# Transposing one operand of a two-layer graph network on VectorE and the DMA engines instead of TensorE

## The chip, the cores and the metric

The kernel runs on one core of one Trainium2 chip. The metric is the device time of one execution in microseconds (us). Each figure below is the median of a kernel's timed executions.

## The reference, cut to what matters

```python
# x, adj: (32, 512, 512) fp32; 32 independent batches; nodemask: (32, 512)
# layer 0
h   = relu(layernorm(x))
agg = (adj @ h) / max(rowsum(adj), 1e-6)
x   = x + relu(concat([h, agg]) @ W0.T)          # W0: (512, 1024)
# layer 1
h   = relu(layernorm(x))
q, k = split(h @ Wqk);  v = h @ Wv
agg = adj @ (k * mask)
w   = mask * rowdot(q, agg) / sqrt(512)
x   = x + softmax(w over the 512 rows)[:, None] * v
```

## The kernel before

Each batch has six 512 x 512 x 512 products, under names that every profile line uses. Layer 0: **y** = h0 W2, and **o** = h0 W1 + A y, which is two products summed in one accumulation. Layer 1: **z** = A (h1 mask), **q** = h1 (Wq Wk^T), whose row-dot with z gives the attention weight, and **v** = h1 Wv. A is the adjacency with its rows divided by their sums.

A product is not done plainly. It is one step of the Strassen-Winograd scheme: 7 parts on 256-wide blocks instead of 8, at the price of sums of blocks. Four sums on VectorE prepare the left operand (their results are called `hT_s`, `aT_s`, `h1T_s`), and four prepare the right one (`h1m_t`, `y_t`):

```python
class Left:                         # tt = one VectorE tensor_tensor, 128x512
    ...
    tt(s1, a21, a22, ALU.add)       # first sum
    tt(a21, a11, a21, ALU.subtract) # second, in place
    tt(s2, s1, a11, ALU.subtract)   # third
    tt(s4, a12, s2, ALU.subtract)   # fourth
    self.p = {1: a11, 2: a12, 3: s4, 4: a22, 5: s1, 6: s2, 7: a21}
```

The parts run in the order 1, 6, 7, 5, 2, 4, 3. **Part 1 needs no sum; part 6, the second, needs the third sum.** After parts 6 and 7 VectorE makes u2 and u3 out of PSUM, and the later parts wait for those.

The kernel gives TensorE its left operands transposed. All three (h0 as `hT`, A as `aT`, h1 as `h1T`) are transposed on TensorE in 128 x 128 tiles, sixteen an operand (1.83 us of TensorE for h1's sixteen; `pth`, `pta`, `pt` are their PSUM tiles), and ScalarE copies them out (four copies of 128 x 512 an operand, 595 ns each):

```python
def transpose_block(dst, src, c, func, name):
    p = ps_t.tile([P, 4, P], F32, tag="t", name=name)
    for d in range(4):
        nc.tensor.transpose(p[:, d, :], src[:, ts(d, P)], ident)
    nc.scalar.activation(dst[:, :, ts(c, P)], p, func)
```

The loop is software-pipelined over the batches:

```python
for i in range(B + 1):
    layer0_y(i)
    transpose_h1(i - 1); mask_h1(i - 1)
    layer1_z(i - 1)
    transpose_adj(i)
    load_a(i + 1)                         # DMA of the next adj
    XN[0, i + 1] = layer_norm(i + 1)      # statistics on VectorE, power on GpSimd
    between = layer1_q(i - 1)
    layer0_out(i, between)
    transpose_h(i + 1); normalize_adj(i + 1)
    layer1_v(i - 1)
    load_x(i + 2)
    # (conditions for the first and last batches cut)
```

The source order is not the order in which an engine runs its instructions. A scheduler orders each engine's queue when the kernel is compiled, and what stands in front in a queue can hold up what stands behind: below, VectorE stays idle for 2.66 us before a sum whose operand is late, while sums whose operands have landed stand behind it.

Of the kernel before, what the change touches and what calls it, by code (L numbers as in the profile page):

```python
# [10 lines left out]
F32 = mybir.dt.float32  # L11
# [4 lines left out]
P = 128  # L16
# [6 lines left out]
def kernel(  # L23
# [42 lines left out]
    class Left:  # L66


        def __init__(self, t, name, tag):
            s = big.tile([P, 3, 2, H], F32, tag=tag, bufs=1, name=f"{name}_s")  # L70
            a11, a12, a21, a22 = block(t, 0, 0), block(t, 1, 0), block(t, 0, 1), block(t, 1, 1)
            s1, s2, s4 = s[:, 0], s[:, 1], s[:, 2]
            tt(s1, a21, a22, ALU.add)
            tt(a21, a11, a21, ALU.subtract)
            tt(s2, s1, a11, ALU.subtract)
            tt(s4, a12, s2, ALU.subtract)
            self.p = {1: a11, 2: a12, 3: s4, 4: a22, 5: s1, 6: s2, 7: a21}
# [15 lines left out]
    def product(name, pairs, sink, between=()):  # L93


        between = list(between)

        def part(k, bank, first):
            n = 0
            for rc in range(2):  # L100
                for left, right in pairs:
                    for dc in range(2):
                        nc.tensor.matmul(  # L103
                            bank[:, rc, :], left.p[k][:, dc, ts(rc, P)], right.p[k][:, dc, :],
                            start=(first and n == 0), stop=(n == 4 * len(pairs) - 1),
                            skip_group_check=True,
                        )
                        n += 1
            if between:
                between.pop(0)()  # L110

        def bank(k):
            return ps_m.tile([P, 2, H], F32, tag="m", name=f"p{name}_{k}")

        def temp(tag, bufs):
            return big.tile([P, 2, H], F32, tag=tag, bufs=bufs, name=f"{tag}{name}")

        p1 = bank(1)
        part(1, p1, True)
        s1 = temp("s1", 1)  # L120
        nc.scalar.activation(s1, p1, AF.Copy)  # L121
        p6 = bank(6)
        part(6, p6, True)
        u2 = temp("u2", 2)
        tt(u2, p6, s1, ALU.add)
        p7 = bank(7)
        part(7, p7, True)
        u3 = temp("u3", 2)
        tt(u3, p7, u2, ALU.add)
        p5 = bank(5)  # L130
        part(5, p5, True)
        sink(1, 1, p5, u3)
        part(2, p1, False)
        sink(0, 0, p1, None)
        part(4, p7, False)
        sink(1, 0, p7, u2)
        part(3, p5, False)
        sink(0, 1, p5, u2)
        for f in between:
            f()  # L140
# [6 lines left out]
                tt(block(dst, r, c), p, u, ALU.add)  # L147
        return sink

    def transpose_block(dst, src, c, func, name):  # L150

        p = ps_t.tile([P, 4, P], F32, tag="t", name=name)
        for d in range(4):
            nc.tensor.transpose(p[:, d, :], src[:, ts(d, P)], ident)  # L154
        nc.scalar.activation(dst[:, :, ts(c, P)], p, func)  # L155

    X, A, XN, HT, AT, Y, H1T, H1M, Z, DEGM, SM = ({} for _ in range(11))

    def load_x(b):
        X[b] = tile4("x", 3, f"x_{b}")  # L160
# [14 lines left out]
    load_x(0)  # L175
    w_in = []
    for half, tag, bufs in (
        (w0[:, 0:F], "x", 3), (w0[:, F:2 * F], "x", 3), (wqk[:, 0:F], "c", 3), (wqk[:, F:2 * F], "c", 3),
    ):
        t = tile4(tag, bufs, f"w_in{len(w_in)}")  # L180
        nc.sync.dma_start(out=t, in_=half.rearrange("(c p) f -> p c f", p=P))  # L181
        w_in.append(t)
# [13 lines left out]
    def layer_norm(b, name):  # L196

        mv = small.tile([P, C, 2], F32, tag="mv", name=f"mv{name}")
        rstd = small.tile([P, C], F32, tag="rstd", name=f"rstd{name}")
        for c in range(C):  # L200
            st = small.tile([P, 6], F32, tag="st", bufs=4, name=f"st{name}_{c}")
            nc.vector.bn_stats(st, X[b][:, c, :])  # L202
            nc.vector.bn_aggr(mv[:, c, :], st)
        nc.vector.tensor_scalar(rstd, mv[:, :, 1], LN_EPS, None, op0=ALU.add)  # L204
        nc.gpsimd.tensor_tensor(rstd, rstd, mhalf, op=ALU.pow)  # L205
        xn = tile4("xn", 2, f"xn{name}")
        for c in range(C):
            nc.vector.tensor_scalar(  # L208
                xn[:, c, :], X[b][:, c, :], mv[:, c, 0:1], rstd[:, c:c + 1],
                op0=ALU.subtract, op1=ALU.mult,  # L210
            )
        return xn

    def normalize_adj(b):
        deg = small.tile([P, C], F32, tag="deg", name=f"deg_{b}")
# [7 lines left out]
            nc.scalar.activation(A[b][:, c, :], A[b][:, c, :], AF.Copy, scale=rdeg[:, c:c + 1])  # L223

    def transpose_h(b):
        t = tile4("hT", 1, f"hT_{b}")
        xn = XN.pop((0, b))
        for c in range(C):
            transpose_block(t, xn[:, c, :], c, AF.Relu, f"pth_{b}_{c}")
        HT[b] = Left(t, f"hT_{b}", "hTs")  # L230

    def transpose_adj(b):
        t = tile4("aT", 1, f"aT_{b}")
        an = A.pop(b)
        for c in range(C):
            transpose_block(t, an[:, c, :], c, AF.Copy, f"pta_{b}_{c}")
        AT[b] = Left(t, f"aT_{b}", "aTs")

    def transpose_h1(b):
        t = tile4("h1T", 1, f"h1T_{b}")  # L240
        xn = XN[1, b]
        for c in range(C):
            transpose_block(t, xn[:, c, :], c, AF.Relu, f"pt1_{b}_{c}")
        H1T[b] = Left(t, f"h1T_{b}", "h1Ts")

    def mask_h1(b):
        t = tile4("h1m", 1, f"h1m_{b}")
        xn = XN[1, b]
        for c in range(C):
            nc.vector.tensor_scalar(t[:, c, :], xn[:, c, :], 0.0, mcol[:, c, b:b + 1], op0=ALU.max, op1=ALU.mult)  # L250
        H1M[b] = Right(t, f"h1m_{b}", big, "h1mt")

    def layer0_y(b):
        y = tile4("c", 3, f"y_{b}")
        product(f"y_{b}", [(HT[b], w2)], store_in(y))
        Y[b] = Right(y, f"y_{b}", big, "yt")

    def layer0_out(b, between):
        def sink(r, c, p, u):
            xb = block(X[b], r, c)  # L260
            if u is not None:
                t = big.tile([P, 2, H], F32, tag="pre", bufs=2, name=f"pre_{b}_{r}{c}")
                tt(t, p, u, ALU.add)
                p = t
            nc.vector.scalar_tensor_tensor(xb, p, 0.0, xb, op0=ALU.max, op1=ALU.add)

        product(f"o_{b}", [(HT.pop(b), w1), (AT[b], Y.pop(b))], sink, between)
        XN[1, b] = layer_norm(b, f"1_{b}")

    def layer1_z(b):  # L270
        Z[b] = tile4("c", 3, f"z_{b}")
        product(f"z_{b}", [(AT.pop(b), H1M.pop(b))], store_in(Z[b]))

    def layer1_q(b):

        q = tile4("c", 3, f"q_{b}")
        product(f"q_{b}", [(H1T[b], m)], store_in(q))
        z = Z.pop(b)
        w = small.tile([P, C], F32, tag="w", name=f"w_{b}")
        for c in range(C):  # L280
            nc.vector.scalar_tensor_tensor(
                q[:, c, :], q[:, c, :], 1.0, z[:, c, :], op0=ALU.mult, op1=ALU.mult, accum_out=w[:, c:c + 1],
            )
        nc.vector.tensor_tensor(w, w, DEGM.pop(b), op=ALU.mult)
        top = small.tile([P, 1], F32, tag="top", name=f"top_{b}")
        nc.vector.tensor_reduce(top, w, AX.X, ALU.max)
# [26 lines left out]
        return [lambda: None, lambda: None, maximum, spread, total]  # L313

    def layer1_v(b):
        v = tile4("c", 3, f"v_{b}")
        product(f"v_{b}", [(H1T.pop(b), w3)], store_in(v))
        xo, sm = X.pop(b), SM.pop(b)
        for c in range(C):
            nc.vector.scalar_tensor_tensor(  # L320
                xo[:, c, :], v[:, c, :], sm[:, c:c + 1], xo[:, c, :], op0=ALU.mult, op1=ALU.add
            )
        nc.sync.dma_start(out=out[b].rearrange("(c p) f -> p c f", p=P), in_=xo)


    XN[0, 0] = layer_norm(0, "0_0")
    mcol = const.tile([P, C, B], F32, name="mcol")
    pmk = ps_t.tile([P, C, B], F32, tag="t", name="pmk")
    for c in range(C):
# [2 lines left out]
    transpose_h(0)  # L332
    for t, dst in zip(w_in, (w1T, w2T, wqT, wkT)):
        for c in range(4):
            transpose_block(dst, t[:, c, :], c, AF.Copy, f"ptw_{dst.name}_{c}")
    for d in range(D):
        p = ps_m.tile([P, 512], F32, tag="m", name=f"pm_{d}")
        for a in range(D):
# [10 lines left out]
    for i in range(B + 1):  # L349
        between = []  # L350
        if i < B:
            layer0_y(i)
        if i > 0:
            transpose_h1(i - 1)
            mask_h1(i - 1)
            XN.pop((1, i - 1))
            layer1_z(i - 1)
        if i < B:
            transpose_adj(i)
        if i + 1 < B:  # L360
            load_a(i + 1)
            XN[0, i + 1] = layer_norm(i + 1, f"0_{i + 1}")
        if i > 0:
            between = layer1_q(i - 1)
        if i < B:
            layer0_out(i, between)
        else:
            for f in between:
                f()
        if i + 1 < B:  # L370
            transpose_h(i + 1)
            normalize_adj(i + 1)
        if i > 0:
            layer1_v(i - 1)
        if i + 2 < B:
            load_x(i + 2)
# [28 lines left out]
```

## Time and profile before

| kernel before | value | how to read it |
|---|---|---|
| time | 2618.59 us | median of 4 |
| TensorE busy | 98% of the span | it sets the end |
| VectorE, ScalarE busy | 63%, 18% | room on average, which says nothing about the moment |
| granted TensorE clock | 0.999 | no throttle in the loop |
| one batch | 79.89 us | from one `pta` to the next |

The prediction shows the page, the chain and the timeline. From the view of waits it used one more line (columns: who waits for whom, us in total, times, longest):

```profile
PE pv L103 <- DVE u3v L64: 22.5, 31, 0.8
```

Within the loop this is the only wait of TensorE that recurs: 0.73 us a batch, once in v. The last adjacency transposes and q's parts follow one another with no gap.

### The profile page before, as it was taken

The page shows a single profiled execution, that of the slowest core. Times are in us where ns is not written, and L with a number is a line of the kernel's source. Part 1 is how long each engine was busy: PE and PEld are TensorE (multiplying, and loading weights), DVE is VectorE, ACT ScalarE, POOL GpSimd, SP SyncE. Part 2 cuts the span into 40 slices and gives each one's busy share as a digit, 9 for nine tenths or more (in the row PEclk, how much of TensorE's full clock was granted, in tenths as well). Part 3 has the DMA queues.
Part 4 walks back from the last instruction along what each step waited for, and adds up shares of the span by engine and source line. Part 5 has one row for each costly group of instructions (what it writes and reads, how often), then busy time and mean ns, then how long its engine had stood idle before and what let it go on. Part 6 is the DMA issues. An engine that isn't in the chain of part 4 may idle for free.

```text
span 2616.5 us, 30420 instructions
## 1 busy us (share of the span) xinstructions
PE 2559.3 (98%) x12548; PEld 2218.6 (85%) x12548; DVE 1647.6 (63%) x3282; ACT 481.6 (18%) x854; POOL 74.3 (3%) x70
## 2 busy tenths in 40 slices
PE   6999999999999999999999999999999999999998
PEld 4888888888888888888888888888888888888887
DVE  4766567666576665676665766656766657666555
ACT  2211212111121112121111211121211112111211
POOL 0000000000000000000000000000000000000000
PEclk9999999999999999999999999999999999999999
DMA  4100111010111000110101110011101011100000
GB/s 146 33 33 30 35 49 49 33 49 17 49 49 49 33 33 33 49 49 33 49 17 49 49 49 33 33 33 49 49 33 49 17 49 49 49 33 33 33 17 33
DMA packets 53514, 107.91 MB, mean 41 GB/s; under 512 B 1632, under 2 KB 1632, under 8 KB 53376
## 3 DMA queue, kind: packets, MB, share of 16 engines
q1 hardware_dynamic: 53376, 105.98, 11.7%
q8 instruction: 98, 1.61, 0.3%
q14 instruction: 40, 0.33, 0.0%
HBM read 72.42 MB, written 33.55 MB: 41 GB/s over the span
## 4 chain that ended last, share of the span: by engine, by line
PE 97%; DVE 1%; DMA 0%; SPq 0%; ACT 0%; issue 0%; POOL 0%; POOLq 0%; DVEq 0%
PE po L103 30%; PE pz L103 15%; PE pq L103 15%; PE pv L103 15%; PE py L103 15%; PE pth L154 2%; PE pta L154 2%; PE pt L154 2%; DVE u3v L64 1%; PE pm L339 1%; DMA mask_sb<-in_nodemask_dram 0%; PE pbc L297 0%; DVE st L202 0%; SPq L181 0%; PE psum L307 0%
## 5 line engine op out<-in xcount | busy, mean ns | idle before, releaser
L103 PE MATMUL po<-w1T,hT 128*128 128x256 f32 x768 | 200.5, 383 | 0.0
L103 PE MATMUL po<-y,aT 128*128 128x256 f32 x768 | 197.1, 379 | 0.0
L103 PE MATMUL pv<-wv_sb,h1T 128*128 128x256 f32 x768 | 186.7, 379 | 0.0
L103 PE MATMUL pq<-m_sb,h1T 128*128 128x256 f32 x768 | 186.6, 379 | 0.0
L103 PE MATMUL pz<-h1m,aT 128*128 128x256 f32 x768 | 186.6, 379 | 0.0
L103 PE MATMUL py<-w2T,hT 128*128 128x256 f32 x768 | 181.7, 379 | 0.7 <-ACT s1y L121 0.7
L202 DVE BATCH_NORM_STATS2 st<-x 128x6 f32<-128x512 f32 x256 | 166.8, 674 | 9.6 <-DMA x<-in_x_dram 8.1
L208 DVE TENSOR_SCALAR xn<-x,mv,rstd 128x512 f32<-128x512 f32 x256 | 122.6, 543 | 66.3 <-POOL rstd L205 66.3
L103 PEld LDWEIGHTS py<-w2T,hT 128*128 128x128 f32 x768 | 145.7, 190 | 21.3 <-ACT s1y L121 1.1
L103 PEld LDWEIGHTS po<-y,aT 128*128 128x128 f32 x768 | 145.9, 190 | 19.8
L103 PEld LDWEIGHTS po<-w1T,hT 128*128 128x128 f32 x768 | 143.2, 190 | 18.6
L103 PEld LDWEIGHTS pv<-wv_sb,h1T 128*128 128x128 f32 x768 | 141.2, 190 | 16.7
L103 PEld LDWEIGHTS pq<-m_sb,h1T 128*128 128x128 f32 x768 | 141.1, 190 | 16.6
L103 PEld LDWEIGHTS pz<-h1m,aT 128*128 128x128 f32 x768 | 141.0, 190 | 16.6
L205 POOL TENSOR_TENSOR rstd<-rstd,mhalf 128x4 f32<-128x4 f32 x64 | 73.6, 1151 | 2488.5 <-DVE rstd L204 2488.5
L64 DVE TENSOR_TENSOR pre<-po,u2o 128x512 f32<-128x512 f32 x64 | 44.3, 692 | 149.9 <-PE po L103 149.9
L103 PE MATMUL po<-w_t,hT_s 128*128 128x256 f32 x512 | 131.5, 379 | 0.0
L103 PE MATMUL po<-y_t,aT_s 128*128 128x256 f32 x512 | 131.4, 379 | 0.0
L155 ACT ACTIVATE hT<-pth 128x512 f32<-128x512 f32 x128 | 69.8, 595 | 334.5 <-PE pth L154 334.4
L103 PE MATMUL pv<-wv_t,h1T_s 128*128 128x256 f32 x512 | 121.1, 379 | 0.0
L103 PE MATMUL pz<-h1m_t,aT_s 128*128 128x256 f32 x512 | 121.0, 379 | 0.0
L103 PE MATMUL pq<-m_t,h1T_s 128*128 128x256 f32 x512 | 121.0, 379 | 0.0
(151 smaller groups left out, 4389.3 us busy)
## 6 DMA issues: line engine op xcount, KB each, us to landing
x<-in_x_dram SPq DMA_DIRECT2D x32, 1024.0 KB, 5.3
adj<-in_adj_dram SPq DMA_DIRECT2D x32, 1024.0 KB, 5.2
out_dram<-x SPq DMA_DIRECT2D x32, 1024.0 KB, 4.3
w_in<-in_L_gnn_W_dram SPq DMA_DIRECT2D x2, 1024.0 KB, 9.0
w_in<-in_L_gnn_Wqk_dram SPq DMA_DIRECT2D x2, 1024.0 KB, 13.1
wv_sb<-in_L_gnn_Wv_dram SPq DMA_DIRECT2D x1, 1024.0 KB, 14.4
mask_sb<-in_nodemask_dram SPq DMA_DIRECT2D x1, 64.0 KB, 12.0
```

Of the source, the lines that this page charges most:

```text
L64: nc.vector.tensor_tensor(o, a, b, op=op)
L103: nc.tensor.matmul(bank[:, rc, :], left.p[k][:, dc, ts(rc, P)], right.p[k][:, dc, :], start=(first and n == 0), stop=(n == 4 * len(pairs) ...
L154: nc.tensor.transpose(p[:, d, :], src[:, ts(d, P)], ident)
L155: nc.scalar.activation(dst[:, :, ts(c, P)], p, func)
L202: nc.vector.bn_stats(st, X[b][:, c, :])
L205: nc.gpsimd.tensor_tensor(rstd, rstd, mhalf, op=ALU.pow)
L208: nc.vector.tensor_scalar(xn[:, c, :], X[b][:, c, :], mv[:, c, 0:1], rstd[:, c:c + 1], op0=ALU.subtract, op1=ALU.mult,)
L339: nc.tensor.matmul(p, wqT[:, a, ts(d, P)], wkT[:, a, :], start=(a == 0), stop=(a == D - 1))
```

## The change

Its intent is to take h1's sixteen transposes off TensorE, the bound. VectorE transposes h1 within 32 x 32 blocks, in place, in four instructions of 128 x 512. Then sixteen DMAs of 64 KB move the blocks between the four groups of 32 partitions. To pay for the new work on VectorE, ScalarE takes over the normalization (one activation with scale, bias and relu). q and v are no longer stored; they are consumed block by block out of PSUM. The first two edits of the diff only address the transposed operands in a new layout, in which the first index is the block of rows; it holds for all three.

```diff
-            a11, a12, a21, a22 = block(t, 0, 0), block(t, 1, 0), block(t, 0, 1), block(t, 1, 1)
+            a11, a12, a21, a22 = block(t, 0, 0), block(t, 0, 1), block(t, 1, 0), block(t, 1, 1)
...
-                            bank[:, rc, :], left.p[k][:, dc, ts(rc, P)], right.p[k][:, dc, :],
+                            bank[:, rc, :], left.p[k][:, rc, ts(dc, P)], right.p[k][:, dc, :],
...
+    def turn(t, src, name, how):
+        if how == "pe":
+            for c in range(C):
+                transpose_block(t[:, c, :].rearrange("p (d n) -> p d n", d=4), src[:, c, :], f"{name}_{c}")
+            return
+        for c in range(C):
+            nc.vector.transpose(src[:, c, :], src[:, c, :])
+        s16, t16 = (u.rearrange("p c (d n) -> p (c d) n", n=P) for u in (src, t))
+        for q in range(4):
+            for r in range(4):
+                nc.sync.dma_start(out=t16[ts(q, 32), :, ts(r, 32)], in_=s16[ts(r, 32), :, ts(q, 32)])
...  # layer_norm
-            nc.vector.tensor_scalar(
-                xn[:, c, :], X[b][:, c, :], mv[:, c, 0:1], rstd[:, c:c + 1],
-                op0=ALU.subtract, op1=ALU.mult,
-            )
+            nc.scalar.activation(h[:, c, :], X[b][:, c, :], AF.Relu, bias=nb[:, c:c + 1], scale=rstd[:, c:c + 1])
...  # transpose_h and transpose_adj: turn(..., "pe"); transpose_h1:
+            nc.vector.tensor_scalar(hm[:, c, :], h[:, c, :], mcol[:, c, b:b + 1], None, op0=ALU.mult)
         t = tile4("h1T", 1, f"h1T_{b}")
-        for c in range(C):
-            transpose_block(t, xn[:, c, :], c, AF.Relu, f"pt1_{b}_{c}")
+        turn(t, h, f"pt1_{b}", "dma")
+        H1M[b] = Right(hm, f"h1m_{b}", big, "h1mt")
         H1T[b] = Left(t, f"h1T_{b}", "h1Ts")
...  # q and v: the sink multiplies each block with z, or adds it to x, in 256-wide pieces
```

(The changes in the numbers of buffers are cut.)

More of the change, by code (lines that the diff above doesn't have):

```diff
@@ L66, with __init__ @@
     class Left:
-        def __init__(self, t, name, tag):
-            s = big.tile([P, 3, 2, H], F32, tag=tag, bufs=1, name=f"{name}_s")
-            a11, a12, a21, a22 = block(t, 0, 0), block(t, 1, 0), block(t, 0, 1), block(t, 1, 1)
+        def __init__(self, t, name, tag, bufs=1):
+            s = big.tile([P, 3, 2, H], F32, tag=tag, bufs=bufs, name=f"{name}_s")
+            a11, a12, a21, a22 = block(t, 0, 0), block(t, 0, 1), block(t, 1, 0), block(t, 1, 1)
             s1, s2, s4 = s[:, 0], s[:, 1], s[:, 2]
@@ L123, in product @@
         part(6, p6, True)
-        u2 = temp("u2", 2)
+        u2 = temp("u2", 1)
         tt(u2, p6, s1, ALU.add)
@@ L127, in product @@
         part(7, p7, True)
-        u3 = temp("u3", 2)
+        u3 = temp("u3", 1)
         tt(u3, p7, u2, ALU.add)
@@ L148, in store_in, with transpose_block @@
         return sink
-    def transpose_block(dst, src, c, func, name):
+    def transpose_block(dst, src, name):
         p = ps_t.tile([P, 4, P], F32, tag="t", name=name)
@@ L154, in transpose_block @@
             nc.tensor.transpose(p[:, d, :], src[:, ts(d, P)], ident)
-        nc.scalar.activation(dst[:, :, ts(c, P)], p, func)
-    X, A, XN, HT, AT, Y, H1T, H1M, Z, DEGM, SM = ({} for _ in range(11))
+        nc.scalar.activation(dst, p, AF.Copy)
+    def turn(t, src, name, how):
[9 more added lines that the diff above has]
+                nc.sync.dma_start(out=t16[ts(q, 32), :, ts(r, 32)], in_=s16[ts(r, 32), :, ts(q, 32)])
+    X, A, HN, HT, AT, Y, H1T, H1M, Z, DEGM, SM = ({} for _ in range(11))
     def load_x(b):
@@ L177 @@
     for half, tag, bufs in (
-        (w0[:, 0:F], "x", 3), (w0[:, F:2 * F], "x", 3), (wqk[:, 0:F], "c", 3), (wqk[:, F:2 * F], "c", 3),
+        (w0[:, 0:F], "x", 3), (w0[:, F:2 * F], "x", 3), (wqk[:, 0:F], "c", 2), (wqk[:, F:2 * F], "c", 2),
     ):
@@ L205, in layer_norm @@
         nc.gpsimd.tensor_tensor(rstd, rstd, mhalf, op=ALU.pow)
-        xn = tile4("xn", 2, f"xn{name}")
+        nb = small.tile([P, C], F32, tag="nb", name=f"nb{name}")
+        nc.vector.scalar_tensor_tensor(nb, mv[:, :, 0], -1.0, rstd, op0=ALU.mult, op1=ALU.mult)
+        h = tile4("h", 2, f"h{name}")
         for c in range(C):
-            nc.vector.tensor_scalar(
-                xn[:, c, :], X[b][:, c, :], mv[:, c, 0:1], rstd[:, c:c + 1],
-                op0=ALU.subtract, op1=ALU.mult,
-            )
-        return xn
+            nc.scalar.activation(h[:, c, :], X[b][:, c, :], AF.Relu, bias=nb[:, c:c + 1], scale=rstd[:, c:c + 1])
+        return h
     def normalize_adj(b):
@@ L225, in transpose_h @@
     def transpose_h(b):
-        t = tile4("hT", 1, f"hT_{b}")
-        xn = XN.pop((0, b))
-        for c in range(C):
-            transpose_block(t, xn[:, c, :], c, AF.Relu, f"pth_{b}_{c}")
-        HT[b] = Left(t, f"hT_{b}", "hTs")
+        t = tile4("hT", 2, f"hT_{b}")
+        turn(t, HN.pop((0, b)), f"pth_{b}", "pe")
+        HT[b] = Left(t, f"hT_{b}", "hTs", 2)
     def transpose_adj(b):
         t = tile4("aT", 1, f"aT_{b}")
-        an = A.pop(b)
-        for c in range(C):
-            transpose_block(t, an[:, c, :], c, AF.Copy, f"pta_{b}_{c}")
+        turn(t, A.pop(b), f"pta_{b}", "pe")
         AT[b] = Left(t, f"aT_{b}", "aTs")
     def transpose_h1(b):
+        h = HN.pop((1, b))
+        hm = tile4("h1m", 1, f"h1m_{b}")
+        for c in range(C):
+            nc.vector.tensor_scalar(hm[:, c, :], h[:, c, :], mcol[:, c, b:b + 1], None, op0=ALU.mult)
         t = tile4("h1T", 1, f"h1T_{b}")
-        xn = XN[1, b]
-        for c in range(C):
-            transpose_block(t, xn[:, c, :], c, AF.Relu, f"pt1_{b}_{c}")
+        turn(t, h, f"pt1_{b}", "dma")
+        H1M[b] = Right(hm, f"h1m_{b}", big, "h1mt")
         H1T[b] = Left(t, f"h1T_{b}", "h1Ts")
-    def mask_h1(b):
-        t = tile4("h1m", 1, f"h1m_{b}")
-        xn = XN[1, b]
-        for c in range(C):
-            nc.vector.tensor_scalar(t[:, c, :], xn[:, c, :], 0.0, mcol[:, c, b:b + 1], op0=ALU.max, op1=ALU.mult)
-        H1M[b] = Right(t, f"h1m_{b}", big, "h1mt")
     def layer0_y(b):
-        y = tile4("c", 3, f"y_{b}")
+        y = tile4("c", 2, f"y_{b}")
         product(f"y_{b}", [(HT[b], w2)], store_in(y))
@@ L261, in sink @@
             if u is not None:
-                t = big.tile([P, 2, H], F32, tag="pre", bufs=2, name=f"pre_{b}_{r}{c}")
+                t = big.tile([P, 2, H], F32, tag="pre", bufs=1, name=f"pre_{b}_{r}{c}")
                 tt(t, p, u, ALU.add)
@@ L267, in layer0_out, with sink @@
         product(f"o_{b}", [(HT.pop(b), w1), (AT[b], Y.pop(b))], sink, between)
-        XN[1, b] = layer_norm(b, f"1_{b}")
+        HN[1, b] = layer_norm(b, f"1_{b}")
     def layer1_z(b):
-        Z[b] = tile4("c", 3, f"z_{b}")
+        Z[b] = tile4("c", 2, f"z_{b}")
         product(f"z_{b}", [(AT.pop(b), H1M.pop(b))], store_in(Z[b]))
     def layer1_q(b):
-        q = tile4("c", 3, f"q_{b}")
-        product(f"q_{b}", [(H1T[b], m)], store_in(q))
         z = Z.pop(b)
+        wc = small.tile([P, C, 2], F32, tag="wc", name=f"wc_{b}")
+        def sink(r, c, p, u):
+            t = big.tile([P, 2, H], F32, tag="pre", bufs=1, name=f"preq_{b}_{r}{c}")
+            if u is not None:
+                tt(t, p, u, ALU.add)
+                p = t
+            zb = block(z, r, c)
+            for rc in range(2):
+                nc.vector.scalar_tensor_tensor(
+                    t[:, rc, :], p[:, rc, :], 1.0, zb[:, rc, :], op0=ALU.mult, op1=ALU.mult,
+                    accum_out=wc[:, 2 * r + rc, c:c + 1],
+                )
+        product(f"q_{b}", [(H1T[b], m)], sink)
         w = small.tile([P, C], F32, tag="w", name=f"w_{b}")
-        for c in range(C):
-            nc.vector.scalar_tensor_tensor(
-                q[:, c, :], q[:, c, :], 1.0, z[:, c, :], op0=ALU.mult, op1=ALU.mult, accum_out=w[:, c:c + 1],
-            )
+        nc.vector.tensor_tensor(w, wc[:, :, 0], wc[:, :, 1], op=ALU.add)
         nc.vector.tensor_tensor(w, w, DEGM.pop(b), op=ALU.mult)
@@ L315, in layer1_v, with sink @@
     def layer1_v(b):
-        v = tile4("c", 3, f"v_{b}")
-        product(f"v_{b}", [(H1T.pop(b), w3)], store_in(v))
         xo, sm = X.pop(b), SM.pop(b)
-        for c in range(C):
-            nc.vector.scalar_tensor_tensor(
-                xo[:, c, :], v[:, c, :], sm[:, c:c + 1], xo[:, c, :], op0=ALU.mult, op1=ALU.add
-            )
+        def sink(r, c, p, u):
+            if u is not None:
+                t = big.tile([P, 2, H], F32, tag="pre", bufs=1, name=f"prev_{b}_{r}{c}")
+                tt(t, p, u, ALU.add)
+                p = t
+            xb = block(xo, r, c)
+            for rc in range(2):
+                k = 2 * r + rc
+                nc.vector.scalar_tensor_tensor(
+                    xb[:, rc, :], p[:, rc, :], sm[:, k:k + 1], xb[:, rc, :], op0=ALU.mult, op1=ALU.add
+                )
+        product(f"v_{b}", [(H1T.pop(b), w3)], sink)
         nc.sync.dma_start(out=out[b].rearrange("(c p) f -> p c f", p=P), in_=xo)
-    XN[0, 0] = layer_norm(0, "0_0")
+    HN[0, 0] = layer_norm(0, "0_0")
     mcol = const.tile([P, C, B], F32, name="mcol")
@@ L334 @@
         for c in range(4):
-            transpose_block(dst, t[:, c, :], c, AF.Copy, f"ptw_{dst.name}_{c}")
+            transpose_block(dst[:, :, ts(c, P)], t[:, c, :], f"ptw_{dst.name}_{c}")
     for d in range(D):
@@ L354 @@
             transpose_h1(i - 1)
-            mask_h1(i - 1)
-            XN.pop((1, i - 1))
             layer1_z(i - 1)
@@ L361 @@
             load_a(i + 1)
-            XN[0, i + 1] = layer_norm(i + 1, f"0_{i + 1}")
+            HN[0, i + 1] = layer_norm(i + 1, f"0_{i + 1}")
         if i > 0:
```

## The prediction

(In it, 684 to 692 are the nanoseconds that VectorE is busy with one fp32 tensor_tensor of 128x512 in the trace before, and the transpose put at 0.60 us is VectorE's block transpose.)

> **What bounds the kernel now.** I read the page first (engine totals, the 40 slices), then the chain of work that ended last over one steady batch, then the timeline of that batch, then the waits and the DMA table.
>
> ```profile
> PE 2559.3 (98%) x12548; PEld 2218.6 (85%) x12548; DVE 1647.6 (63%) x3282; ACT 481.6 (18%) x854; POOL 74.3 (3%) x70
> PEclk9999999999999999999999999999999999999999
> q1 hardware_dynamic: 53376, 105.98, 11.7%
> ```
>
> TensorE has work for 98% of the span at full clock, VectorE for 63%, and the DMA engines stand idle nine tenths of the time. So TensorE sets the end, and a microsecond taken off it counts, provided that nothing makes it wait. The chain over one batch shows how little it waits (columns: start, length, what):
>
> ```profile
> 1000.37 0.87 PE pta L154 x8
> 1001.24 0.43 PE pq L103 x2
> 1001.67 0.96 PE pta L154 x8
> 1002.64 11.66 PE pq L103 x54
> ...
> 1049.80 0.69 DVE u3v L64
> 1050.48 0.04 issue
> 1050.53 3.72 PE pv L103 x16
> 1054.25 12.09 PE py L103 x56
> 1066.33 0.87 PE pt L154 x8
> 1067.21 0.43 PE pz L103 x2
> 1067.64 0.96 PE pt L154 x8
> 1068.60 11.66 PE pz L103 x54
> 1080.26 0.87 PE pta L154 x8
> ```
>
> From one pta to the next is 1080.26 - 1000.37 = 79.89 us; 32 such are 2556 of the 2618 us. A one-pair product (y, z, q, v) is 28 tile products in 12.09 us, so one of its seven parts is 1.73 us. Two items are what the change can win: the 16 h1 transposes, 0.87 + 0.96 = 1.83 us a batch, and TensorE's wait in v for VectorE's u3v, 0.69 + 0.04 = 0.73 us. What it can lose I read from the timeline just after the adjacency transposes:
>
> ```profile
> 1002.18 1.08 ACT L155 ACTIVATE aT<-pta 128x512 f32<-128x512 f32 x2 [0.26 <-PE pta L154]
> 1003.30 0.69 DVE L64 TENSOR_TENSOR aT_s<-aT 128x512 f32<-128x512 f32 x1 [2.21 <-ACT aT L155]
> 1003.77 1.89 PE L103 MATMUL pq<-m_t,h1T_s 128*128 128x256 f32 x8
> 1005.36 0.69 DVE L64 TENSOR_TENSOR aT_s<-aT,aT_s 128x512 f32<-128x512 f32 x1
> ...
> 1070.18 0.69 DVE L64 TENSOR_TENSOR h1T_s<-h1T 128x512 f32<-128x512 f32 x1
> 1073.19 0.69 DVE L64 TENSOR_TENSOR h1T_s<-h1T,h1T_s 128x512 f32<-128x512 f32 x1
> ```
>
> The four sums of h1T (h1T_s) are made during z, 1070.2 to 1073.9, some 10 us before q's second part reads them. The sums of aT come after the last aT copy, in q, and nothing in q reads them. Keep that order in mind.
>
> [...] the trace has 684 to 692 (0.61 us start to start, 0.72 where it waits for the one before). [...] no transpose of that kind is in the trace before, so I estimate 0.60 us start to start for 128x512, as for a tensor_tensor. [...] here 11.7% of 16 x 2616.5 us over 53376 packets is 91.8 ns for a packet of 1986 B, [...]
>
> **The change, part by part.** I used the compiled order of each engine of both kernels.
>
> Off TensorE: 16 transposes a batch, -1.83 us on the path.
>
> VectorE: normalizing xn leaves it (8 x 0.48 = 3.8 us a batch) for ScalarE, which has room (18%). Four block transposes come (2.4 us), and q and v are consumed in 256-wide pieces out of PSUM, about the old work. In the stretch before u3v the four xn (1.92 us) and one mask go, so u3v ends an estimated 1.3 us before TensorE wants it: -0.73 us on the path.
>
> DMA: 16 moves of 64 KB, each 512 runs of 128 B, 32 on each of 16 engines, all on the queue that carries x, adj and out. Call V the end of v. I add up VectorE's queue to the fourth block transpose (h1m, x pieces, sums at the durations above) and get V + 3. The queue's order is two moves, out (which waits for the last x piece, V + 5), two moves, the next x (which waits for out to land, 4.3 us more, V + 9.5), then twelve moves, then adj. [...]
>
> Who waits? z ends at V + 24.2. Then the order turns against the change. VectorE's queue now has the h1T sums **after the aT sums**, not in z; q's second part waits for the third h1T sum. Let Z be the first pta matmul (1000.20 above). aT's last copy ends and the aT sums start at Z + 3.1. ScalarE now also has the next batch's four normalizations in front of the aT copies: counting from the BN statistics over POOL's power (1.0 to 1.3 us), the last of them ends at about Z + 1.5 where the first copy used to start at Z + 0.64. I take half of that delay, 0.45 us, since the statistics may come earlier. So: aT sums from Z + 3.55, four of 0.73, 0.61, 0.72, 0.61 = 2.67, to Z + 6.2; three h1T sums, 0.73 + 0.61 + 0.69 = 2.03, to Z + 8.25; the second part starts at Z + 8.3. It started at 1003.77 = Z + 3.57. That is **+4.75 us a batch on the path**, a gap of 3 to 4 us in TensorE after q's first part. The moves have until Z + 6.2 = V + 30 to land, [...] so this wait hides them, and hides too that the row sums of the next adj now stand ahead of u2q.
>
> Sum: -1.83 - 0.73 + 4.75 = +2.19 us; 31 batches in the loop +68 us. In the last batch no y lies between v and z, so the moves are exposed: [...] and z also waits for the late h1m sums; I put +8 us. 2618 + 68 + 8 = 2694 us.
>
> **The rivals.**
> Moves hidden, no new wait: if the sums' order costs nothing, the gain is 2.56 x 31 = 79 us, 2540 us. For it: DMA is idle and VectorE has slack on average. Against it: the compiled order, and VectorE having to catch up within one part of q.
> The DMA is the wait: [...] One chance in four.
> VectorE late in y: the last h1m sums and u3y come with about 1 us to spare (V + 7.6 against V + 8.6). If the block transpose takes 1.2 us and not 0.6, y waits 1.4 us: +43 us.
> Clock: [...]
>
> **Range and chances.** The order of sums is certain, its size good to 1 us a batch (31 us): 2660 to 2725 without the rivals. The DMA and clock rivals stretch the upper side; an earlier aT copy or more overlap the lower. Range 2640 to 2820. The mark for 2% slower is 2671, so slower 0.73, within 2% 0.2, faster 0.07.
>
> **What would show it.** Right: a wait of about 3 to 4 us a time, 31 times, of TensorE's q for VectorE's h1T_s; the h1T sums after the aT sums; no wait of v for u3v; no pt transposes; moves landed before the h1T sums start; a period near 82.1 us. Wrong if VectorE's h1T_s waits for DMA for several us (the second rival), if q starts its second part within 2 us of its first (the first rival), if y or z gain waits for VectorE, or if the clock falls below 0.99.

## More of the kernel before

The kernel before took 2618.59 us in the rounds that timed it against the change (2617.97 to 2619.01, four executions), and a median of 2618.2 to 2619.2 us in the rounds of the experiments, which ran on three chips.

## The result, and the profile after

The changed kernel took **2732.77 us** (2728.02 to 2735.64, four executions) against 2618.59. The ratio is 1.0434, with a 95% interval of 1.0416 to 1.0452: slower. Every ratio here is the mean time of one kernel's runs over that of the other's in the same rounds, so it is not quite the ratio of the medians. The predicted figure was 2694 with a range of 2640 to 2820; the direction and the range held, and the middle was 39 us too low.

The page of the changed kernel (engines with busy time and instructions; the DMA queue with packets, MB and share; the group of q's matmuls that read the h1T sums with busy time, mean ns, and idle time before them):

```profile
PE 2551.6 (94%) x12036; PEld 2203.6 (81%) x12036; DVE 1669.6 (61%) x3634; ACT 557.0 (20%) x918; POOL 73.6 (3%) x70
...
q1 hardware_dynamic: 323712, 139.57, 20.2%
...
L104 PE MATMUL pq<-m_t,h1T_s 128*128 128x256 f32 x512 | 155.5, 457 | 114.0 <-DVE h1T_s L64 114.0
```

The transposes are gone: 12548 - 12036 = 512 = 32 x 16 instructions fewer. Yet TensorE's busy time fell by only 7.7 us, and it is busy for 94% of the span, not 98%. The third line says why, twice. These matmuls were preceded by 114.0 us of idle time, put down to VectorE's h1T_s. And one of them took 457 ns on average, where the page of the kernel before has 379 (121.0 us busy, no idle before). The granted clock of the profiled run is 0.980.

Its waits (columns as above):

```profile
PE pq L104 <- DVE h1T_s L64: 114.0, 31, 4.1
...
PE pta L155 <- ACT aT L156: 21.6, 31, 1.1
PE pq L104 <- DMA h1T<-h: 3.3, 1, 3.3
```

The recurring wait of v for u3v has gone. In its place stand one of 3.7 us a batch on VectorE and one of 0.7 us a batch on ScalarE. The wait for a DMA came once, in the last batch.

Its timeline around one such wait, and the same place one batch later (columns: start, length, engine, line, what, and in brackets the idle time before it and what ended it):

```profile
1036.07 1.04 PE L155 MATMUL pta<-ident,adj 128*128 128x128 f32 x8
...
1037.81 1.14 PE L155 MATMUL pta<-ident,adj 128*128 128x128 f32 x8 [0.70 <-ACT aT L156]
1038.50 1.09 ACT L156 ACTIVATE aT<-pta 128x512 f32<-128x512 f32 x2 [0.27 <-PE pta L155]
...
1038.78 1.91 PE L104 MATMUL pq<-m_sb,h1T 128*128 128x256 f32 x8
...
1039.62 0.69 DVE L64 TENSOR_TENSOR aT_s<-aT 128x512 f32<-128x512 f32 x1 [2.66 <-ACT aT L156]
...
1042.28 0.69 DVE L64 TENSOR_TENSOR h1T_s<-h1T 128x512 f32<-128x512 f32 x1
...
1043.61 0.69 DVE L64 TENSOR_TENSOR h1T_s<-h1T_s,h1T 128x512 f32<-128x512 f32 x1
...
1044.35 3.54 PE L104 MATMUL pq<-m_t,h1T_s 128*128 128x256 f32 x8 [3.67 <-DVE h1T_s L64]
...
1127.76 1.99 PE L104 MATMUL pq<-m_t,h1T_s 128*128 128x256 f32 x8 [3.66 <-DVE h1T_s L64]
```

Read it downwards. q's part 1 starts at 1038.78, and part 6 could follow it. But VectorE stands idle for 2.66 us until the last aT copy is there, then makes the four aT sums, and only then the h1T sums that part 6 needs. Part 6 starts at 1044.35, which is 8.28 us after the first `pta` at 1036.07. Part 6 then takes 3.54 us in this batch and 1.99 us in the next one. The gap before it is the same in both.

The table of stretches over those two parts (columns: stretch, length, then busy time and number of instructions of TensorE, its weight loads, VectorE, ScalarE and GpSimd, then the granted clock, the DMA share and GB/s):

```profile
1044.30:1047.80 3.50, 3.45 (x9) 2.77 (x10) 3.23 (x4) 0.13 (x1) 0.00 (x0) 0.54 0.00 0
1127.70:1131.20 3.50, 3.44 (x16) 3.05 (x17) 3.40 (x6) 0.12 (x1) 0.00 (x0) 1.00 0.00 0
```

After the first gap the clock is 0.54 and TensorE gets through 9 matmuls; after the second it is 1.00 and 16 get through. Part 6 was slow (2.6 to 3.8 us) in 18 of the 30 batches in which I could match it.

The moves are innocent in this picture. The timeline of the queue that issues the DMAs shows the last twelve of a batch:

```profile
1021.66 9.51 SPq L170 DMA_DIRECT2D h1T<-h  x12
```

They are issued by 1031.2 and take 3.1 us (median) from issue to landing. From 1033 on the DMA engines are idle, and the first h1T sum starts at 1042.28, some 9 us later.

### The profile page after: what moved, and what is told of

It reads as the page before. It is cut to its first block, busy times and chain, and to the rows that moved or that the text cites. A ratio compares the mean times of both kernels' runs of the same rounds, so it can differ in the third digit from the quotient of the medians. Undisturbed runs are those within 1.5% of the kernel's fastest.

```text
span 2726.2 us, 30919 instructions
## 1 busy us (share of the span) xinstructions
PE 2551.6 (94%) x12036; PEld 2203.6 (81%) x12036; DVE 1669.6 (61%) x3634; ACT 557.0 (20%) x918; POOL 73.6 (3%) x70
## 2 busy tenths in 40 slices
DMA packets 323858, 141.53 MB, mean 52 GB/s; under 512 B 271968, under 2 KB 271968, under 8 KB 323712
## 3 DMA queue, kind: packets, MB, share of 16 engines
q1 hardware_dynamic: 323712, 139.57, 20.2%
## 4 chain that ended last, share of the span: by engine, by line
PE 75%; DVE 14%; ACT 6%; issue 2%; POOL 1%; DMA 1%; SPq 1%; DVEq 0%; POOLq 0%
PE po L104 29%; PE pq L104 14%; PE py L104 14%; PE pv L104 13%; ACT h L225 3%; DVE st L217 2%; DVE y_t L64 2%; PE pth L155 2%; ACT aT L156 2%; DVE aT_s L64 2%; DVE h1T_s L64 1%; DVE y L64 1%; POOL rstd L220 1%; PE pta L155 1%; DVE h1T L64 1%
## 5 line engine op out<-in xcount | busy, mean ns | idle before, releaser
L104 PE MATMUL pq<-m_t,h1T_s 128*128 128x256 f32 x512 | 155.5, 457 | 114.0 <-DVE h1T_s L64 114.0
L225 ACT ACTIVATE h<-x,nb,rstd 128x512 f32<-128x512 f32 x256 | 190.7, 804 | 320.6 <-DVE nb L222 320.6
L104 PEld LDWEIGHTS pq<-m_t,h1T_s 128*128 128x128 f32 x512 | 114.6, 230 | 145.2 <-DVE h1T_s L64 121.9
L104 PE MATMUL po<-w1T,hT 128*128 128x256 f32 x768 | 200.5, 383 | 0.0
L104 PE MATMUL pq<-m_sb,h1T 128*128 128x256 f32 x768 | 196.4, 402 | 3.3 <-DMA h1T<-h 3.3
L104 PE MATMUL po<-y,aT 128*128 128x256 f32 x768 | 197.1, 379 | 0.0
L104 PE MATMUL pv<-wv_sb,h1T 128*128 128x256 f32 x768 | 186.7, 379 | 0.0
L104 PE MATMUL pz<-h1m,aT 128*128 128x256 f32 x768 | 181.5, 379 | 0.7 <-ACT s1z L122 0.7
L104 PE MATMUL py<-w2T,hT 128*128 128x256 f32 x768 | 181.7, 379 | 0.4 <-ACT s1y L122 0.4
L104 PEld LDWEIGHTS pq<-m_sb,h1T 128*128 128x128 f32 x768 | 155.2, 205 | 28.0 <-issue 3.7
L104 PEld LDWEIGHTS pz<-h1m,aT 128*128 128x128 f32 x768 | 145.8, 190 | 20.9 <-ACT s1z L122 1.1
L104 PEld LDWEIGHTS py<-w2T,hT 128*128 128x128 f32 x768 | 145.7, 190 | 20.7 <-ACT s1y L122 0.6
L104 PEld LDWEIGHTS po<-y,aT 128*128 128x128 f32 x768 | 145.9, 190 | 19.8
L104 PEld LDWEIGHTS po<-w1T,hT 128*128 128x128 f32 x768 | 143.2, 190 | 18.6
L104 PEld LDWEIGHTS pv<-wv_sb,h1T 128*128 128x128 f32 x768 | 141.2, 190 | 16.7
L64 DVE TENSOR_TENSOR pre<-po,u2o 128x512 f32<-128x512 f32 x64 | 44.3, 692 | 149.9 <-PE po L104 149.9
L104 PE MATMUL po<-w_t,hT_s 128*128 128x256 f32 x512 | 131.5, 379 | 0.0
L104 PE MATMUL po<-y_t,aT_s 128*128 128x256 f32 x512 | 131.4, 379 | 0.0
L237 ACT ACTIVATE adj<-adj,rdeg 128x512 f32<-128x512 f32 x128 | 82.0, 711 | 202.7 <-DVE rdeg L233 197.9
```

Source lines behind the costliest of these rows:

```text
L64: nc.vector.tensor_tensor(o, a, b, op=op)
L104: nc.tensor.matmul(bank[:, rc, :], left.p[k][:, rc, ts(dc, P)], right.p[k][:, dc, :], start=(first and n == 0), stop=(n == 4 * len(pairs) ...
L225: nc.scalar.activation(h[:, c, :], X[b][:, c, :], AF.Relu, bias=nb[:, c:c + 1], scale=rstd[:, c:c + 1])
L237: nc.scalar.activation(A[b][:, c, :], A[b][:, c, :], AF.Copy, scale=rdeg[:, c:c + 1])
```

## The experiments

Line numbers shift between the kernels: L104, L115 and L117 are the same matmul in the products, and L64 is VectorE's sum in all. The theory on trial is that **the order of VectorE's queue** makes the loss, with the clock on top; the rivals are the moves and small packets, VectorE's load, and ScalarE's queue. Where an edit fixes an order, it uses this helper. It adds a dependency without a semaphore, so it changes only where the scheduler puts an instruction:

```python
def latest():                       # the instruction emitted last
    return nc.cur_bb.bb.instructions[-1]
def behind(ins, earlier):
    tc.add_manual_dep(ins, earlier.name,
        mybir.DependencyInfo(mybir.DependencyClass.NoSync, mybir.DependencyReason.DATA), reason="order")
```

### h1_pe: h1 transposed on TensorE again, all else as changed

```diff
-        turn(t, h, f"pt1_{b}", "dma")
+        turn(t, h, f"pt1_{b}", "pe")
```

> Undoes one part: h1 is transposed on TensorE again (16 transposes a batch), the rest of the change stays. Theory (the loss is the late h1T sums in q and the clock drop after the gap): in the compiled order the h1T sums are back in z, so q has no gap; 1.83 us of transposes come back, v's wait for u3v (0.73 us) stays away, and ScalarE's normalizations still delay the aT copies by some 0.4 us. Period 79.89 - 0.73 + 0.4 = 79.6 us, time about 2610 us, range 2600 to 2625, clock 0.99 or more. Rival (the loss comes from the other parts of the change, normalizing on ScalarE and consuming q and v by blocks): it stays above 2690 us.

Measured: 2632.57 us (2632.0 to 2634.78), ratio 1.0053 (1.0038 to 1.0068), clock 0.998, result correct. Of the 114 us lost, 100 are gone, so the loss comes with this part of the change. The figure still missed my expectation by some 20 us. Its waits name the reason:

```profile
PE pta L155 <- ACT aT L156: 38.5, 29, 2.4
...
DVE st L217 <- DMA x<-in_x_dram: 32.1, 30, 5.3
```

TensorE waits 1.3 us a batch for the aT copies. On ScalarE the next batch's four normalizations stand ahead of those copies. They come late partly because the statistics wait 1.1 us a batch for x. This cost is not of the moves but of the normalization on ScalarE, and the experiment h1_pe_norm below isolates it.

### sums_first: the h1T sums ahead of the aT sums

```diff
         AT[b] = Left(t, f"aT_{b}", "aTs")
+        if b > 0:
+            behind(AT[b].first, H1T[b - 1].last)   # first aT sum behind the last h1T sum
```

> The changed kernel with one edge more: VectorE's first aT sum must stand behind the last h1T sum. Theory: q's second part no longer waits (the wait of PE for h1T_s falls from 114 us to under 10), the moves have long landed, and the clock stays up. But the scheduler then puts the row sums of the next adj, which wait for their load (some 5.3 us after the last pta), between the aT sums and u2q, so q's fourth-bank part waits about 2.4 us for u3q. Period 77.33 + 0.9 + 2.4 = 80.6 us, time about 2650 us, range 2620 to 2670. Rival (the DMA moves are the limit): h1T_s now waits for the moves instead and the time stays above 2700 us.

Measured: 2665.16 us (2655.16 to 2670.3), ratio 1.0172 (1.0145 to 1.0199), clock 0.988, correct. The wait for h1T_s has gone, as the theory has it, and 68 us with it, without touching a move. But a new wait came up behind it:

```profile
PE pq L117 <- DVE u3q L64: 63.9, 30, 3.0
...
DVE deg L244 <- DMA adj<-in_adj_dram: 131.1, 32, 9.2
```

The row sums of the next adj (`deg`) stand ahead of u2q in VectorE's queue, and they wait 4.1 us a batch for adj to land. In the changed kernel VectorE came to `deg` so late that adj was there.

### sums_deg: the same, and the row sums of adj behind q

```diff
         nc.vector.tensor_reduce(deg, A[b], AX.X, ALU.add)
+        if "top" in MARK:
+            behind(latest(), MARK["top"])     # "top": q's last reduction on VectorE
```

> sums_first with one more edge: the row sums of the next adj stand on VectorE behind q's last use. Theory: TensorE's wait in q for u3q (64 us in sums_first) goes and with it the clock drop; what is left over the best case is the wait for the aT copies, 0.9 to 1.2 us a batch, and some 10 us at the end: 2575 to 2600 us. Rival (VectorE or DMA holds q up in yet another place): above 2620 us.

Measured: 2564.06 us (2562.38 to 2567.25), ratio 0.9794 (0.9777 to 0.981), clock 0.999, correct. Two order edges, with every move, every block transpose and every instruction of the change in place, are worth 2732.8 - 2564.1 = 168.7 us. They turn the change from 4.3% slower into 2.1% faster, so neither the moves nor VectorE's load makes the loss. It came out 11 us better than the low end of my expectation. The largest recurring wait of TensorE left is the one for ScalarE:

```profile
PE pta L168 <- ACT aT L169: 22.5, 31, 1.3
```

### fill: eight useless tile products in the gap

This kernel leaves the order alone and keeps TensorE working while it waits.

```diff
+        def filler():                                   # run after q's part 1
+            p = ps_t.tile([P, H], F32, tag="t", name=f"pfill_{b}")
+            for n in range(8):
+                nc.tensor.matmul(p, ident, m_sb[:, n % 4, 0:H], start=(n == 0), stop=(n == 7))
-        product(f"q_{b}", [(H1T[b], m)], sink)
+        product(f"q_{b}", [(H1T[b], m)], sink, [filler])
```

(Order edges that hold the eight in a row between parts 1 and 6 are cut.)

> The changed kernel with 8 useless tile products (8 x 0.43 = 3.44 us, identity times m, into a bank that nobody reads) put into the gap after q's first part, in place of idle time. Clock theory (TensorE's idle gap of 3.67 us makes its clock fall to half for some us, which costs about 40 us in all): the gap shrinks to some 0.2 us, the granted clock rises above 0.99, the second part of q takes 1.9 us and not up to 3.8 us in every batch, and the time falls by 40 us to about 2692 us. Rival (the slow second parts come from operands being read while VectorE or DMA write, not from idleness): the slow parts stay and the time stays at 2733 us or grows.

Measured: 2690.2 us (2688.48 to 2691.53), ratio 1.0271 (1.0256 to 1.0287), clock 0.999, correct. Its timeline at the same place:

```profile
1023.65 3.62 PE L315 MATMUL pfill<-m_sb,ident 128*128 128x256 f32 x16
1027.48 1.99 PE L115 MATMUL pq<-m_t,h1T_s 128*128 128x256 f32 x8 [0.21 <-DVE h1T_s L64]
```

The gap is 0.2 us, part 6 is slow in none of 31 batches, and 27 of 30 batches follow the one before at 81.86 or 81.87 us. Part 6 still waits for the same sum, so the useless work gains nothing but the clock. The difference is 2732.8 - 2690.2 = 42.6 us. In the last batch, which has no such gap, the useless products lengthen the path: from q's part 1 to its part 7 it is 8.67 us here and 5.22 in the changed kernel. So the throttled clock costs the changed kernel some 42.6 + 3.4 = 46 us.

### fill2: two useless products, a shorter gap

```diff
-            for n in range(8):
+            for n in range(2):
```

> fill with 2 useless tile products (0.86 us) in place of 8, so that a gap of 2.8 us stays. [...] clock 0.99 or more and 2685 to 2700 us, as with 8. Rival (every idle microsecond costs clock in proportion): slow second parts remain, clock about 0.985 and 2705 to 2725 us.

Measured: 2695.83 us (2692.5 to 2700.24), ratio 1.0295 (1.028 to 1.0311), clock 0.993, correct. Time and clock lie inside what I expected. But the clock did not stay up in every batch. The timeline shows the shortened gap:

```profile
1040.58 1.99 PE L115 MATMUL pq<-m_t,h1T_s 128*128 128x256 f32 x8 [2.79 <-DVE h1T_s L64]
```

With 2.8 us left, part 6 was slow (2.6 to 3.8 us) in 6 of 30 batches (the first of them after 3.1 us); with 3.67 us it was 18 of 30. In sums_first, at a clock of 0.988, the part that waits for u3q was slow in 17 of 30 batches, after gaps of 1.9 to 3.0 us. So gaps from 1.9 us up were followed by a slow part in these runs.

The trace of the changed kernel shows which gaps do it there. In its clock record each of the 21 stretches at half clock starts on a grid of 3.413 us. Four cells of this grid (columns as in the table of stretches above):

```profile
2033.99:2037.40 3.41, 1.39 (x7) 0.88 (x5) 3.02 (x5) 0.88 (x2) 0.00 (x0) 1.00 0.75 225
2037.40:2040.82 3.42, 1.77 (x4) 1.51 (x5) 3.35 (x5) 0.00 (x0) 0.00 (x0) 0.50 0.21 83
...
1204.55:1207.96 3.41, 1.41 (x7) 0.90 (x5) 3.00 (x5) 0.90 (x2) 0.00 (x0) 1.00 0.65 206
1207.96:1211.38 3.42, 1.76 (x8) 1.58 (x9) 3.35 (x5) 0.00 (x0) 0.00 (x0) 1.00 0.29 106
```

Both gaps are 3.67 us long. TensorE was busy for 1.39 us in the first cell, and the clock was 0.50 in the next; it was busy for 1.41 us in the third, and the clock stayed at 1.00. So it goes through this whole trace after the first 45 us: of 752 cells at full clock, the 20 with at most 1.39 us of work are followed by half clock and the others are not. The border is read from this one trace. (The ends of matmuls in the profile are modelled, so a busy time or a gap may be off by a little.) In this trace it thus counts how a gap falls into the grid, and not only its length. An undisturbed batch of 81.86 us is 24 cells less 0.06 us, so the next gap falls at nearly the same place, and batches without a throttle come mostly two or three in a row.

### rows_late: four whole-row moves, the h1T sums kept late

Its output is wrong, which doesn't matter for the time. Blocks go to the wrong partitions. The aim is to take the 128 B packets away and keep the order.

```diff
-        for q in range(4):
-            for r in range(4):
-                nc.sync.dma_start(out=t16[ts(q, 32), :, ts(r, 32)], in_=s16[ts(r, 32), :, ts(q, 32)])
+        for q in range(4):
+            nc.sync.dma_start(out=t[ts(q, 32)], in_=src[ts(q, 32)])
...
+            behind(H1T[b - 1].first, AT[b].last)    # h1T sums behind the aT sums
```

> Wrong result on purpose: the 16 moves between quadrants are replaced by 4 moves of whole rows (8 KB runs, the same bytes, data not transposed), and VectorE's h1T sums are held behind the aT sums as in the changed kernel. Theory (the moves land about 9 us before the first h1T sum, so their number and packet size cost nothing): still a gap of 3.6 to 4.1 us before q's second part in each batch, and a time within 1% of the changed kernel, 2705 to 2760 us. Rival (small packets or the queue of 16 issues hold something up): the time falls by more than 2%.

Measured: 2634.94 us (2634.12 to 2636.54), ratio 1.0062 (1.0047 to 1.0077), clock 0.999. That is far below what the theory expected, and read naively it says that the small packets cost 98 us. The waits and the order of TensorE's queue say otherwise:

```profile
PE pq L117 <- DVE h1T_s L64: 42.2, 31, 1.4
```

The wait is still for the same sum, not for a DMA, but it is 1.4 us a time. With the other moves the scheduler had **reordered TensorE's queue**: q's part 2, which needs no sum, now runs ahead of the waiting part 6. The edit changed two things at once, so the run decides nothing about packets. It does show that less of the wait remains, and no throttle, if other work stands in the gap. (Part 2 itself waits 0.7 us a batch for ScalarE's copy of part 1, 23.1 us in all.)

### rows_pinned: the same, with TensorE's order pinned

(The line that marks the last `pta` transpose is cut.)

```diff
+                        if name[0] == "q":          # each matmul of q behind the one before,
+                            if "pe" in MARK:        # the first behind the last pta transpose
+                                behind(latest(), MARK["pe"])
+                            MARK["pe"] = latest()
```

> Wrong result on purpose, and the test that rows_late should have been: 4 moves of whole rows in place of 16 moves between quadrants, with VectorE's h1T sums behind the aT sums and TensorE's q matmuls pinned to the changed kernel's order (in rows_late the scheduler put q's second-bank part, which needs no sum, ahead of the waiting part). Theory (moves off the path, order alone sets the wait): gap of 3.6 to 3.8 us before q's part 6 in each batch, clock 0.98, 2720 to 2745 us. Rival (the small packets or 16 issues cost part of the gain): 2690 us or less with a smaller gap.

Measured: 2731.47 us (2727.99 to 2737.94), ratio 1.0433 (1.0418 to 1.0449), clock 0.978. Its output is wrong, which doesn't matter for the time.

```profile
PE pq L117 <- DVE h1T_s L64: 112.3, 32, 4.1
```

With four DMAs of 256 KB, whose rows are far longer than 128 B, in place of sixteen of 64 KB, and with TensorE's order held, the time is the changed kernel's, 1.0433 against 1.0434, down to the wait and the throttle (part 6 slow in 19 of 31). The rival of the small packets falls.

### h1_pe_norm: h1 on TensorE, and the normalization behind the aT copies

```diff
         turn(t, A.pop(b), f"pta_{b}", "pe")
+        MARK["aT"] = latest()                       # the last aT copy on ScalarE
...
             nc.scalar.activation(h[:, c, :], X[b][:, c, :], AF.Relu, bias=nb[:, c:c + 1], scale=rstd[:, c:c + 1])
+            if name[0] == "0" and "aT" in MARK:
+                behind(latest(), MARK["aT"])
```

> h1_pe with ScalarE's normalizations of the next batch behind the aT copies, as in best: the fair kernel to hold best against, for it keeps everything but the moves and the block transposes. If the order of ScalarE's queue is what made h1_pe slower than the kernel before, TensorE's wait for aT (39 us) falls below 10 us and the time drops to 2590 to 2605 us: 0.73 us a batch under the kernel before, for the wait for u3v that stays away. best is then lower by the 16 transposes, 1.83 x 32 = 59 us. Rival (normalizing on ScalarE or the consumption by blocks costs in another way): it stays at 2615 us or more.

Measured: 2588.02 us (2587.85 to 2588.49), ratio 0.9885 (0.9868 to 0.9901), clock 1.000, correct. That is 2 us below the range that I had expected. TensorE has no recurring wait left. Against h1_pe the order of ScalarE's queue is worth 2632.6 - 2588.0 = 44.6 us. This is also the change without its moves: normalization on ScalarE and q and v by blocks, in a good order, are worth 30 us against the kernel before, which took 2618.2 us in these rounds.

### best: all three orders, and the last batch on TensorE

This is sums_deg, plus the normalization edge of h1_pe_norm, plus:

```diff
-        turn(t, h, f"pt1_{b}", "dma")
+        turn(t, h, f"pt1_{b}", "dma" if b < B - 1 else "pe")
```

> sums_deg with two more edits: ScalarE's normalizations of the next batch stand behind the aT copies, and the last batch's h1 is transposed on TensorE. Theory: all three waits that the compiled order made are gone; period 77.33 + 0.45 = 77.8 us, 31 x (77.8 - 79.89) = -65 us, time 2545 to 2570 us, 2 to 3% under the kernel before. Rival: the late normalizations make pth wait instead, or VectorE is late in y, and the time stays within 1% of the kernel before.

Measured: **2542.45 us** (2542.38 to 2543.29), ratio 0.9709 (0.9695 to 0.9724), clock 1.000, correct. It beats both kernels: 76 us under the kernel before and 190 us under the changed one, and it lies 3 us below the range that I had expected. Its chain over one batch:

```profile
1010.31 0.87 PE pth L168 x8
...
1048.41 0.45 PE pta L168 x4
...
1048.89 0.61 ACT aT L169
...
...
1050.68 12.10 PE pq L117 x56
...
1087.80 0.87 PE pth L168 x8
```

q runs as one block of 12.10 us without a gap; in the kernel before a product took 12.09. The only thing in the loop's chain that is not TensorE is one aT copy, 0.61 us long, of which TensorE waits 0.25 us (7.5 us in 30 waits). One batch is 1087.80 - 1010.31 = 77.49 us. The kernel before has 79.89, and taking off the two items the prediction named as winnable, 1.83 and 0.73, leaves 77.33.

Against h1_pe_norm, the moves and block transposes in place of TensorE's are worth 2588.0 - 2542.5 = 45.6 us. I had expected 59: sixteen transposes of 1.83 us times 32. But best takes them off in 31 batches, which makes 57. And a batch of h1_pe_norm takes 78.88 us against 77.48 in best (medians of the loop), so 1.40 us of the 1.83 are gained. Of the 0.43 that are missing, 0.25 are the wait for aT here, which h1_pe_norm does not have; the rest I have not taken apart.

| kernel | us | ratio |
|---|---|---|
| before | 2618.6 | 1 |
| changed | 2732.8 | 1.0434 |
| changed, gap filled (fill) | 2690.2 | 1.0271 |
| changed, h1T sums first (sums_first) | 2665.2 | 1.0172 |
| the same, deg behind q (sums_deg) | 2564.1 | 0.9794 |
| all orders, last batch on TensorE (best) | 2542.5 | 0.9709 |

## Why the prediction was right or wrong

**The order of the sums: right, in mechanism and size.** Part 6 was to start at Z + 8.3 and started at Z + 8.28 or 8.29 in 27 of 31 batches (the others from 6.96 to 8.64). (Z, 1000.20 in the prediction, is the first `pta` matmul in the timeline; it does not stand in the lines shown there, whose chain starts at 1000.37.) The aT sums were to start at Z + 3.55, and started at 1039.62 - 1036.07 = 3.55. v's wait for u3v and the `pt` transposes are gone, as foreseen. A batch without throttle takes 81.86 us against a predicted 82.1. Over 31 batches, (81.86 - 79.89) x 31 = 61 us, where the prediction had 68. The experiments sums_first and sums_deg show the cause: changing the order alone removes it.

**The clock: the term that was missing from the sum.** The prediction put it among the rivals and left it out of the sum; the trace of the kernel before, at 0.999, had nothing to size it by. It came in 18 of 30 batches and cost some 46 us (fill). That is the distance between the middle of the prediction and the measurement: without it the kernel is at some 2687, and 2694 was predicted. Also, "wrong if the clock falls below 0.99" came true: 0.980 in the profiled run. How often it comes is what the experiments measured: in 18 of 30 batches with gaps of 3.63 to 4.08 us, and in 6 of 30 with mostly 2.8 us (fill2). In the changed kernel's trace a cell of 3.413 us didn't have to be idle for it: up to about 1.4 us of work in it, 41%, was still followed by a clock of 0.50.

**The first and last batches: nearly right.** What fill costs over the kernel before, 2690.2 - 2618.6 = 71.6, less the 61 of the loop and less the 3.4 of useless products in the last batch, is 7 us; 8 was put down, as the author's estimate. The last batch shows 3.3 us of q waiting for the DMA and 1.9 us of z for h1m_t.

**The moves: hidden, as said.** Both kernels carry the same DMA traffic on this queue apart from the moves, so their packets cost on average (0.202 x 16 x 2726.2 - 0.117 x 16 x 2616.5) / (323712 - 53376) = 14.5 ns of one engine each (the difference is 528 packets a move, 512 runs and 16 more). The kernel before makes no such moves, so its trace could not show this cost; the "one chance in four" that the prediction gave the rival was the author's estimate. At 14.5 ns twelve moves need 12 x 33 x 14.5 ns = 5.7 us of each engine, if they are spread evenly. That is less than the 9.5 us that their issue takes, so the issue is more likely what sets when they land. They landed some 9 us early. rows_pinned shows that coarser moves change nothing.

**The block transpose: right.** It was to be 0.60 us start to start. The trace has 696 ns busy and about 0.60 between starts, and in the loop y doesn't wait for VectorE, so that rival falls.

**ScalarE: the half was right, the reach was not.** The estimated delay of 0.45 us for the aT sums held, as above; taking half of the delay was a guess, and it hit (the first aT copy starts at 1037.18, Z + 1.11, and was at Z + 0.64). But h1_pe_norm and h1_pe show that the same queue costs 44.6 us when h1 stays on TensorE. The prediction saw a delay of the aT sums in it; it did not see that TensorE itself would wait for the aT copies, 0.7 us a batch in the changed kernel.

**The rival "moves hidden, no new wait", at 2540 us**, was right about what the change is worth and wrong about this kernel. It takes three order edges and the last batch's exception to get there: 2542.5 in best. The prediction also saw that the row sums of adj stand ahead of u2q and that the first wait hides them. sums_first uncovered that: removing the first wait gave back only 68 us of what was lost until this second one was moved too.

## What to carry to other kernels

When work moves off the bound engine, compare the compiled order of every queue before and after, not only the busy shares. An operand that now arrives by a slower-looking route may be queued behind work nobody waits for, and an order edge of a few lines is then worth trying first. Remove waits in turn and read the view of waits after each, because a wait that hides another one gives back only part of its cost. And look at the clock after an idle gap on TensorE, for the gap may cost more than its length. Here gaps of 1.9 to 4.1 us were followed in many batches by a slow part (sums_first, fill2, changed kernel): up to 3.78 us in the changed kernel, where a part without throttle takes 1.99. In the changed kernel's trace the clock was 0.50 after each of the 20 cells of 3.41 us with at most 1.39 us of TensorE's work.

## What the runs measured of the hardware

- The clock: in the changed kernel's trace 0.50 after cells with up to 1.39 us of TensorE's work in 3.41 (20 of 752 cells). Gaps of 1.9 to 3.1 us, shorter than a cell, were also followed by slow parts (17 of 30 batches in sums_first, 6 of 30 in fill2).
- Small packets: the 128 B moves held the engines for 3913 us in sum, and the same bytes in 8 KB rows, by the same working, for (0.176 x 16 x 2736.1 - 0.117 x 16 x 2616.5) = 2807 us (rows_pinned): 1.4 times as long, though hidden. A packet of the 128 B moves was 14.5 ns of an engine.
- Issuing a DMA: a move of 64 KB held the issuing queue for 0.63 us (median), where a load of 1 MB held it for 0.37 us; the twelve shown took 9.51 us, more than the 5.7 us that they need of each engine by the estimate above.
- VectorE's fp32 block transpose of 128 x 512: 696 ns, where a tensor_tensor of that size took 683 to 693 ns (the aT sums of the kernel before).
- The order of the compiled queues: worth most of 2732.8 - 2542.5 = 190 us, 168.7 us of it by two edges on VectorE.
